# Edge lists by eighths, source gathers in two parts, longer expert jobs and late weights in a fused Mamba, attention and graph-routed expert kernel

## The chip, the cores and the metric

The kernel runs on one core of a Trainium2 chip. Its time is the device time of one execution in microseconds (us), the median of several runs. TensorE is called PE, VectorE DVE, ScalarE ACT, GpSimd POOL and SyncE SP, as in the profile; PEld is the weight load of PE.

## What is computed

The input x has 4 entries of 32 x 96 tokens (12288 tokens, 96 tiles of 128) with 256 features.

```python
# layer 0
x = x + mamba_d(mamba_t(group_norm(x)))          # selective scans along both axes
# layer 1
t = tokens(x)
t = t + attn(ln(t))      # additive attention inside each entry:
    h = tanh(q[:, :, None, :] + k[:, None, :, :] + bh); e = h @ Wa
    v = softmax(e) @ inputs
t = t + ffn(ln(t))       # a graph decides the experts of each token:
    h = (x @ W_gat).reshape(M, 4, 4); a_src, a_dst = (h*att_src).sum(-1), (h*att_dst).sum(-1)
    e = leaky_relu(a_src[src] + a_dst[dst])
    alpha = softmax of e over the edges of each dst
    agg = segment_sum(h[src] * alpha[:, :, None], dst) + b_gat
    scores = layernorm(agg).reshape(M, 4, 4).mean(1); top 2 of 4, softmax -> gates
    out = sum over experts of gate * (gelu(x @ W1 + b1) @ W2 + b2)
```

There are 1048576 edges with node numbers up to 65536, of which only 12288 are tokens. A source past the last token is read as the last token; edges to a destination past the last token do nothing. Each token also has an edge to itself.

## The kernel before

**Order of the work.** Layer 0 runs in blocks of 384 tokens, 48 slots to a block. When the first entry is through layer 0, the attention of entry 0 begins and is issued between the slots. `Attention.units` (line 866) goes over the tanh columns: 768 to an entry, 3072 in all, each one ACT instruction of 128x3072 (line 905) whose result PE reduces to scores (line 878). Three `th` buffers hold the results; the scores follow two columns behind. Twice per column the generator `steps` (line 2042) is advanced; it issues layer 0 first, and when that has ended, whatever else stands beside the last attention. `after` (line 1062) writes the normalised tokens, the table `tab_s` (20 numbers per token: 4 source scores, 16 features) and per entry `tab_a` (4 destination scores).

**Expert jobs beside layer 0.** `Beside` (line 1563) takes one job per block where `choose` (line 1591) permits: one expert on three half blocks of 256 tokens of an entry whose attention has ended. It uses the idle one of the two `krep` buffers for the weights and `qsel` for one half's input, which is loaded again by `fetch` for each half. The hidden products are issued at slots 0, 3, 5, 8, 10 and 12, the Gelu of all at slot 14 (line 1643), the outputs at slots 15 to 29. Results go to DRAM (`kept`). A unit is one block of 512 tokens by one of the 4 experts; there are 96.

**Edge lists.** `Edges.sort` (line 1192) runs on DVE beside the last attention, by a budget of 2.3 us of its own estimates per tanh column, none in one column of eight. It loads the edges in 32 pieces of 512 columns through two buffers (line 1226), keeps those with a token as destination, and compacts lists with `compact` (line 1138), some 50 short DVE instructions for a list of 384. The edges with both ends among the tokens end in one list of 384 per partition; it is split by four quarters of the destinations (an entry each) into lists of 108 columns. Edges from past the last token are counted by PE products (line 1322) instead. From then on one destination gather of 128 rows per column is issued on POOL (line 1127) for the first three quarters, after a copy that paces POOL (line 771). `Experts.early` (line 1735) does units of the first three entries on PE with a second budget per column, in pairs, by expert. The weights of all four experts, some 4.5 MB, are loaded when the lists are done (line 2069).

**The tail.** After the attention, `tail` (line 1821) issues a plan in half steps, six to an expert unit. For each group of 12 columns POOL gathers the sources (line 1425) and, for the last quarter, the destinations; a marker from DVE keeps POOL from running ahead of its half step (lines 1417 and 1418). `scores` and `values` make the weighted rows; `spread` makes one-hot matrices of the lane and of the quarter's 24 tiles and multiplies the latter by the rows (line 1469, 4 columns at a time); `place` adds them to a quarter's sums in PSUM, one PE product of 480 columns for each gathered column (line 1479). `finish` makes the gates of a quarter. Meanwhile the remaining units run (lines 1723 and 1731). A block whose expert outputs were stored is loaded again once its gates are there (2 MB, line 1881) with its tokens (line 1716), summed with the gates (line 1808) and written (line 1812).

Of the kernel before, what the change touches and what calls it, by code (L numbers as in the profile page):

```python
# [26 lines left out]
P = 128  # L27
# [4 lines left out]
KC = C // P  # L32
# [25 lines left out]
C2, CQ = 384, 108  # L58
# [3 lines left out]
HALVES = 3.0, 9.0  # L62
# [659 lines left out]
class Attention:  # L722
# [4 lines left out]
    def __init__(self, ctx, tc, ident, a, x1, x2, xn2T, tab_s, tab_a):  # L727
        self.nc = nc = tc.nc
        self.ident, self.x1, self.x2, self.xn2T = ident, x1, x2, xn2T
        self.tab_s, self.tab_a = tab_s, tab_a  # L730
# [331 lines left out]
    def after(self, b, t0=0, t1=NT):  # L1062
# [7 lines left out]
        for j in range(j0, N):  # L1070
# [26 lines left out]
            nc.sync.dma_start(self.tab_s[:, n0:n0 + CT, :], hb)  # L1097
            nc.sync.dma_start(self.tab_a[b][:, j * CT:(j + 1) * CT, :], db)
# [5 lines left out]
class Edges:  # L1104
# [6 lines left out]
    def __init__(self, ctx, tc, a, tab_a):  # L1111
        self.nc, self.tc, self.a, self.todo = tc.nc, tc, a, []
        self.tab_a, self.have, self.listed = tab_a, set(), False
        keep = ctx.enter_context(tc.tile_pool(name="el", bufs=1))
        new = lambda name, shape, dt=F32: keep.tile(shape, dt, tag=name, name=name)
        self.cnt = new("cnt", [P, NH])
        self.lost = new("lost", [P, 1])
        self.si, self.di = new("si", [P, 4, CQ], I32), new("di", [P, 4, CQ], I32)
        self.lane, self.tile = new("lane", [P, 4, CQ]), new("tile", [P, 4, CQ])
        self.lanes, self.tiles = new("lanes", [P, P]), new("tiles", [P, NH])  # L1120
        self.gd = new("gd", [P, 4, CQ, HEADS])
        self.nc.sync.dma_start(self.lanes, a["lanes"])

    def gather(self, q, c):
        if (q, c) not in self.have:
            self.have.add((q, c))
            self.nc.gpsimd.indirect_dma_start(  # L1127
                out=self.gd[:, q, c, :], out_offset=None,
                in_=self.tab_a[q].rearrange("p n f -> (p n) f"),
                in_offset=bass.IndirectOffsetOnAxis(ap=self.di[:, q, c:c + 1], axis=0))  # L1130
# [61 lines left out]
    def sort(self):  # L1192
# [4 lines left out]
        with ExitStack() as ctx:  # L1197
            kept = ctx.enter_context(tc.tile_pool(name="ek", bufs=1))
# [3 lines left out]
            with tc.tile_pool(name="es", bufs=1) as lists:  # L1202
# [4 lines left out]
                pair2, pairq, pair3 = new("pair2", C2, F32), new("pairq", C2, F32), new("pair3", 4 * CQ, F32)  # L1207
                over = new("over", 9, F32)
# [10 lines left out]
                with tc.tile_pool(name="ee", bufs=2) as pool:  # L1219
                    for q in range(4):  # L1220
                        for row, to, most in ((1, x, M), (0, s, M - 1)):
                            H = W1 // 4
                            for h in range(4):
# [21 lines left out]
                k1 = new("pair", 2 * W1)[:, :W1]  # L1245
# [3 lines left out]
                x2, _ = self.halves(pair2)  # L1249
                part, tl = w["keep"][:, :C2], w["keep"][:, C2:2 * C2]  # L1250
                for q in range(4):
                    v.tensor_scalar(tl, x2, 7, None, ALU.logical_shift_right)
                    v.tensor_scalar(part, tl, float(P + q * NT), None, ALU.is_ge)
                    v.scalar_tensor_tensor(part, tl, float(P + (q + 1) * NT), part, ALU.is_lt, ALU.mult)
                    v.tensor_copy(pairq, pair2)
                    yield 1.5
                    yield from self.compact(w, part, pairq, CQ, pair3[:, q * CQ:(q + 1) * CQ],
                                            over[:, 5 + q:6 + q])
                v.tensor_reduce(self.lost, over, AX.X, ALU.max)


                n = 4 * CQ
                flat = lambda t: t.rearrange("p q c -> p (q c)")
                x3, s3 = self.halves(pair3)
                lo, hi, d = w["go"][:, :n], w["move"][:, :n], w["bit"][:, :n]
                for of, rows in ((s3, self.si), (x3, self.di)):
                    v.tensor_scalar(d, of, VALID - 1, None, ALU.bitwise_and)
                    v.tensor_scalar(lo, d, P - 1, None, ALU.bitwise_and)
                    v.tensor_scalar(lo, lo, float(NH), None, ALU.mult)
                    v.tensor_scalar(hi, d, 7, None, ALU.logical_shift_right)  # L1270
                    if rows is self.di:
                        v.tensor_scalar(lo, lo, float(NT) / NH, None, ALU.mult)
                        for q in range(1, 4):
                            part = hi[:, q * CQ:(q + 1) * CQ]
                            v.tensor_scalar(part, part, float(-q * NT), 0.0, ALU.add, ALU.max)
                    v.tensor_tensor(flat(rows), lo, hi, ALU.add)
                    yield 1.5
# [4 lines left out]
                self.listed = True  # L1282
# [14 lines left out]
            yield 1.0  # L1297
            p = ctx.enter_context(tc.tile_pool(name="eo", bufs=3))
            ps = ctx.enter_context(tc.tile_pool(name="ep", bufs=1, space=PSUM))
            pc = ps.tile([P, NH], F32, tag="pc", name="pc")  # L1300
            starts = [q * W2 + g for q in range(4) for g in range(0, C1, G1)]
# [32 lines left out]
class Graph:  # L1334
# [85 lines left out]
    def gather(self, j, u):  # L1420
        nc, ed = self.nc, self.ed
        if j not in self.got:
            self.got[j] = self.wk.tile([P, GP, ROW], F32, tag="gs", name="gs", bufs=6)
        q, c0 = divmod(j * GP, CQ)
        nc.gpsimd.indirect_dma_start(  # L1425
            out=self.got[j][:, u, :], out_offset=None, in_=self.tab_s.rearrange("p n f -> (p n) f"),
            in_offset=bass.IndirectOffsetOnAxis(ap=ed.si[:, q, c0 + u:c0 + u + 1], axis=0))
        ed.gather(q, c0 + u)

    def scores(self, j):  # L1430
        nc = self.nc
        gs = self.got.pop(j)
        q, c0 = divmod(j * GP, CQ)
        gd = self.ed.gd[:, q, c0:c0 + GP, :]
        e = self.wk.tile([P, GP, HEADS], F32, tag="e", name="e")
        sh = self.wk.tile([P, GP, HEADS], F32, tag="sh", name="sh")
        v = self.wk.tile([P, GP, ROW], F32, tag="v", name="v", bufs=4)
# [6 lines left out]
        self.got[j], self.v[j] = gs, v  # L1444

    def values(self, j):

        v = self.v[j]
        self.nc.vector.tensor_tensor(
            v[:, :, :HF].rearrange("p n (h x) -> p n h x", x=NEXP),  # L1450
            self.got.pop(j)[:, :, HEADS:].rearrange("p n (h x) -> p n h x", x=NEXP),
            v[:, :, HF:].unsqueeze(3).to_broadcast([P, GP, HEADS, NEXP]), ALU.mult)

    def spread(self, j, g):

        nc, ed = self.nc, self.ed
        q, c0 = divmod(j * GP + g * GG, CQ)
        cols = slice(c0, c0 + GG)
        ol = self.wk.tile([P, GG, P], F32, tag="ol", name="ol")
        oh = self.wk.tile([P, GG, NT], F32, tag="oh", name="oh")  # L1460
        rh = self.wk.tile([P, GG, NT, ROW], F32, tag="rh", name="rh")
        for to, among, which in ((ol, ed.lanes, ed.lane),
                                 (oh, ed.tiles[:, q * NT:(q + 1) * NT], ed.tile)):
            n = to.shape[2]
            nc.vector.tensor_tensor(to, among.unsqueeze(1).to_broadcast([P, GG, n]),
                                    which[:, q, cols].unsqueeze(2).to_broadcast([P, GG, n]),
                                    ALU.is_equal)
        v = self.v[j][:, g * GG:(g + 1) * GG, :]
        nc.vector.tensor_tensor(rh, oh.unsqueeze(3).to_broadcast([P, GG, NT, ROW]),
                                v.unsqueeze(2).to_broadcast([P, GG, NT, ROW]), ALU.mult)  # L1470
        return ol, rh

    def place(self, j, g, ol, rh):
        nc = self.nc
        q, c0 = divmod(j * GP + g * GG, CQ)
        if c0 == 0:
            self.pa[q] = self.ps.tile([P, JB], F32, tag="pa", name="pa")
        for u in range(GG):
            nc.tensor.matmul(self.pa[q][:, :NT * ROW], ol[:, u, :],
                             rh[:, u].rearrange("p n f -> p (n f)"),  # L1480
                             start=(c0 + u == 0), stop=(c0 + u == CQ - 1))
# [81 lines left out]
class Beside:  # L1563
# [5 lines left out]
    PRODUCTS = {0: (0, 0), 3: (0, 1), 5: (1, 0), 8: (1, 1), 10: (2, 0), 12: (2, 1)}  # L1569
    GELU = 14  # L1570
    OUTPUTS = {15: (0, 0), 17: (0, 1), 20: (1, 0), 23: (1, 1), 26: (2, 0), 29: (2, 1)}

    def __init__(self, ctx, tc, a, l0, att, xn2T, dram):
# [7 lines left out]
        n = TOK // self.half // 3  # L1581
# [3 lines left out]
    def units(self):  # L1585

        halves = {(2 * (b * TOK // TB) + 3 * j + k, e) for b, e, j in self.done for k in range(3)}
# [3 lines left out]
    def choose(self, last):  # L1591
# [9 lines left out]
        self.w1, self.w2 = expert_places(place)  # L1601
        rest = att.qsel[(att.entry + 1) % 2]
# [5 lines left out]
        self.first = 2 * (b * TOK // TB) + 3 * j  # L1608
        self.fetch(0)

    def fetch(self, k):
        m = (self.first + k) * self.half
        self.nc.sync.dma_start(self.xt, self.xn2T[:, :, m:m + self.half].rearrange("k p m -> p k m"))

    def __call__(self, slot, last):
        nc = self.nc
        if self.job:
# [3 lines left out]
            if slot - 1 in self.PRODUCTS:  # L1621
                k, f2 = self.PRODUCTS[slot - 1]
                for f in (2 * f2, 2 * f2 + 1):
                    nc.vector.tensor_scalar(self.h[:, k, f, :], self.ps[:, f % 2, :],
# [7 lines left out]
            if slot in self.PRODUCTS:  # L1632
# [6 lines left out]
                if f2 and k < 2:  # L1639
                    self.fetch(k + 1)  # L1640
            if slot == self.GELU:
                h = self.h.rearrange("p k f m -> p (k f m)")
                nc.scalar.activation(h, h, AF.Gelu)
            if slot in self.OUTPUTS:
                k, q = self.OUTPUTS[slot]
                self.ps = self.bank()
                for f in range(FC):
                    nc.tensor.matmul(self.ps[:, 0, :], self.h[:, k, f, q * P:(q + 1) * P],  # L1648
# [15 lines left out]
class Experts:  # L1664
# [25 lines left out]
    def weights(pool, nc, a):  # L1690
        w1 = pool.tile([P, NEXP, KC, FF], F32, tag="w1", name="w1")
        w2 = pool.tile([P, NEXP, FC, C], F32, tag="w2", name="w2")
        for e in range(NEXP):
            nc.sync.dma_start(w1[:, e], a["W1"][e].rearrange("(k p) f -> p k f", p=P))
            nc.sync.dma_start(w2[:, e], a["W2"][e].rearrange("(k p) f -> p k f", p=P))
        b1 = pool.tile([P, NEXP, FC], F32, tag="b1", name="b1")
        nc.sync.dma_start(b1, a["b1"])
# [119 lines left out]
    def outputs_tile(self):  # L1817
        return self.io.tile([P, NQ, NEXP, C], F32, tag="all", name="all")


def tail(tc, a, ed, ex, w, tab_s, tab_a, gates):


    with ExitStack() as ctx:
        gr = Graph(ctx, tc, a, ed, tab_s, tab_a, gates)
# [12 lines left out]
        PQ, PG = CQ // GP, GP // GG  # L1838

        h = free = 0.0  # L1840
        for m in range(4 * PQ):
            q = QUARTERS[m // PQ]
            j = q * PQ + m % PQ
            wide = HALVES[q == B - 1]
            for u in range(GP):
# [344 lines left out]
```

## Time and profile before

| | |
|---|---|
| time, median of 3 runs (lowest, highest) | 15007.42 us (15002.35, 15027.46) |
| the profiled execution, its span | 15006.76 us, 15004.8 us |
| busy: PE, DVE, ACT, POOL | 11632.7, 10437.2, 12227.7, 9042.6 us |
| last tanh of the attention starts | 13868.1 us |
| jobs beside layer 0 (Gelu of line 1643) | 25 of three halves, 5620.8 to 10987.8 us |
| first destination gather | 11883.4 us |
| gathers before and after 13940 us | 324, 540 |
| last gather | 14789.7 us |
| early units, units of the tail | 22, 37 |
| stored blocks loaded in the tail | 19 of 2 MB |

The strips of the page divide the span into 40 slices; a digit is the busy share in tenths. A window answer gives for a stretch its length and the busy time and number of instructions of PE, PEld, DVE, ACT and POOL, then the clock that PE was granted, the share of DMA time and GB/s. A row of a group has the line, the engine, what is written from what, the count, the busy time with the mean in ns, and behind the second bar the idle time of that engine just before these instructions, with what ended it. PE's 4-byte products have two records for each product.

### The profile page before, as it was taken

The page shows a single profiled execution, that of the slowest core. Times are in us where ns is not written, and L with a number is a line of the kernel's source. Part 1 is how long each engine was busy: PE and PEld are TensorE (multiplying, and loading weights), DVE is VectorE, ACT ScalarE, POOL GpSimd, SP SyncE. Part 2 cuts the span into 40 slices and gives each one's busy share as a digit, 9 for nine tenths or more (in the row PEclk, how much of TensorE's full clock was granted, in tenths as well). Part 3 has the DMA queues.
Part 4 walks back from the last instruction along what each step waited for, and adds up shares of the span by engine and source line. Part 5 has one row for each costly group of instructions (what it writes and reads, how often), then busy time and mean ns, then how long its engine had stood idle before and what let it go on. Part 6 is the DMA issues. An engine that isn't in the chain of part 4 may idle for free.

```text
span 15004.8 us, 223310 instructions
## 1 busy us (share of the span) xinstructions
PE 11632.7 (78%) x86496; PEld 5146.9 (34%) x86496; DVE 10437.2 (70%) x14862; ACT 12227.7 (81%) x9485; POOL 9042.6 (60%) x6971
## 2 busy tenths in 40 slices
PE   5676656777777778888887787888877888888888
PEld 2333322222222323333333333333333344433544
DVE  7888887777777877777777877577767633311367
ACT  3454538999999889999999899999988899999121
POOL 5777777777777777767676677477640144100683
PEclk8988978888888888899999889899988999999999
DMA  6777764445454544555454444355531000000224
GB/s 207 227 230 233 239 203 142 150 151 153 150 152 153 161 152 147 152 149 153 150 154 156 149 150 152 105 153 151 152 115 44 15 16 10 24 23 23 59 54 136
DMA packets 1197826, 1986.83 MB, mean 132 GB/s; under 512 B 411984, under 2 KB 645072, under 8 KB 1194320
## 3 DMA queue, kind: packets, MB, share of 16 engines
q1 hardware_dynamic: 1169104, 1967.10, 42.8%
q0 software_dynamic: 27648, 5.36, 0.7%
q8 instruction: 680, 11.14, 0.3%
q14 instruction: 394, 3.23, 0.1%
HBM read 1864.71 MB, written 107.35 MB: 131 GB/s over the span
## 4 chain that ended last, share of the span: by engine, by line
ACT 17%; PE 16%; DVE 7%; POOL 5%; issue 4%; DMA 1%; SPq 0%; DVEq 0%; ACTq 0%; POOLq 0%
ACT th L905 12%; PE pe L878 8%; POOL gs L1425 3%; PE pv L984 3%; ACT dA L410 2%; DVE h L448 1%; ACT pr L968 1%; POOL gd L1127 1%; PE ptw L975 1%; PE po L1731 1%; PE pz L517 1%; PE pc L1322 1%; DVE y L1808 0%; PE ex L1648 0%; DVE dB L423 0%
## 5 line engine op out<-in xcount | busy, mean ns | idle before, releaser
L905 ACT ACTIVATE th<-krep,qsel 128x3072 f32<-128x3072 f32 x3072 | 8667.0, 2847 | 377.0 <-PE pe L878 359.0
L878 PE MATMUL pe<-th,wa_blk 128*32 128x384 f32 x49152 | 5050.1, 539 | 1587.7 <-ACT pr L968 1361.7
L455 POOL TENSOR_TENSOR h<-h,bC 128x768 f32<-128x768 f32 x2048 | 3759.8, 1837 | 2586.0 <-DVE h L448 2187.4
L448 DVE TENSOR_TENSOR_SCAN h<-dA,dB 128x384 f32<-128x384 f32 x3008 | 2707.8, 942 | 988.7 <-ACT dA L410 717.2
L878 PEld LDWEIGHTS pe<-th,wa_blk 128*32 128x32 f32 x49152 | 1459.3, 116 | 4154.1 <-issue 1974.4
L423 DVE TENSOR_TENSOR dB<-bB,dtu 128x768 f32<-128x768 f32 x1912 | 1811.9, 948 | 172.0 <-ACT dtu L498 137.2
L462 POOL TENSOR_TENSOR h<-h 128x768 f32<-128x768 f32 x752 | 1419.6, 1888 | 53.6
L410 ACT ACTIVATE dA<-dt,t_A 128x380 f32<-128x380 f32 x2048 | 1124.7, 570 | 386.2 <-DVE h L448 296.5
L474 PE MATMUL py<-h,ident 128*128 128x384 f32 x2176 | 944.7, 567 | 490.8 <-POOL h L455 490.7
L410 ACT ACTIVATE dA<-dt,d_A 128x372 f32<-128x372 f32 x2048 | 1102.3, 562 | 146.4 <-DVE h L443 107.9
L984 PE MATMUL pv<-xn,pT 128*32 128x257 f32 x18432 | 1101.0, 387 | 129.5 <-DVE pT L977 128.7
L1043 POOL TENSOR_SCALAR sf<-sel,f 128x32 f32<-128x32 f32 x384 | 144.7, 398 | 1583.9 <-ACT f L1039 1481.5
L443 DVE TENSOR_TENSOR_SCAN h<-dA,dB 128x768 f32<-128x768 f32 x544 | 948.3, 1751 | 153.2 <-ACT dA L410 87.7
L977 DVE COPY pT<-ptw 128x512 f32<-128x512 f32 (+1 forms) x768 | 419.3, 546 | 738.3 <-PE ptw L975 737.8
L984 PEld LDWEIGHTS pv<-xn,pT 128*32 128x32 f32 x18432 | 580.2, 111 | 704.9 <-DVE pT L977 256.1
L464 POOL TENSOR_TENSOR y<-y,h 128x384 f32<-128x384 f32 x752 | 783.2, 1042 | 59.0
L463 POOL TENSOR_TENSOR h<-h 128x384 f32<-128x384 f32 x752 | 780.7, 1038 | 58.9
L474 PEld LDWEIGHTS py<-h,ident 128*128 128x128 f32 x2176 | 427.1, 212 | 970.1 <-POOL h L455 740.3
L961 DVE TENSOR_REDUCE nb<-pe 128x1 f32<-128x768 f32 x384 | 362.4, 944 | 405.7 <-PE pe L878 405.6
L1425 POOL DMA_INDIRECT gs<-tab_s,si x432 | 517.5, 1198 | 108.4 <-issue 108.4
L986 DVE COPY pvs<-pv 128x257 f32<-128x257 f32 x384 | 160.7, 419 | 603.4 <-PE pv L984 601.9
L1127 POOL DMA_INDIRECT gd<-tab_a,di x432 | 448.8, 1039 | 185.1 <-issue 182.0
(291 smaller groups left out, 15267.6 us busy)
## 6 DMA issues: line engine op xcount, KB each, us to landing
bB<-bc SPq DMA_DIRECT2D x2048, 384.0 KB
bC<-bc SPq DMA_DIRECT2D x2048, 384.0 KB
all<-kept SPq DMA_DIRECT2D x19, 2048.0 KB
x<-x SPq DMA_DIRECT2D x144, 256.0 KB
x<-x SPq DMA_DIRECT2D x192, 128.0 KB
xt<-xn2T SPq DMA_DIRECT2D x41, 512.0 KB
kept<-ko SPq DMA_DIRECT2D x39, 512.0 KB
qsel<-xn2T SPq DMA_DIRECT2D x75, 256.0 KB
```

The lines of the kernel that those rows point to most:

```text
L410: nc.scalar.activation(inner(dA[:, s * T:(s + 1) * T] if alone else self.dA[s][:, :T]), inner(blk["dt"][:, e, :]), AF.Exp, scale=blk["w"][ ...
L423: nc.vector.tensor_tensor(dB, blk["bB"].pop(j), z["dtu"].unsqueeze(1).to_broadcast([P, SB, T]), ALU.mult)
L443: nc.vector.tensor_tensor_scan(flat(h), dA[:, :SB * T], flat(dB), 0.0, ALU.mult, ALU.add)
L448: nc.vector.tensor_tensor_scan(h[:, s, :], self.dA[s][:, :T], dB[:, s, :], 0.0, ALU.mult, ALU.add)
L455: nc.gpsimd.tensor_tensor(h, h, blk["bC"].pop(j), ALU.mult)
L462: nc.gpsimd.tensor_tensor(h0, h0, h1, ALU.add)
L464: nc.gpsimd.tensor_tensor(y[e], y[e], h0[:, 0, :], ALU.add)
L474: nc.tensor.matmul(z["py"], self.ident, h[:, s, :], start=(i == 0), stop=(i == DS - 1))
L878: nc.tensor.matmul(pe[q * QU:(q + 1) * QU, j, :KQ // 2], self.wa[:, k, :], th[:, c0:c0 + KQ // 2], start=(k == 0), stop=(k == NK - 1))
L905: nc.scalar.activation(th, s["krep"], AF.Tanh, bias=s["qsel"][:, col:col + 1])
L984: nc.tensor.matmul(pv[q * QU:(q + 1) * QU, :C + 1], pT[:, i, q * QU:(q + 1) * QU], s["xn"][:, q * NK + i, :], start=(i == 0), stop=(i == N ...
L1425: nc.gpsimd.indirect_dma_start(out=self.got[j][:, u, :], out_offset=None, in_=self.tab_s.rearrange("p n f -> (p n) f"), in_offset=bass.Ind ...
```

## The change

Five things are changed together.

- The expert jobs beside layer 0 take four halves instead of three: 12 jobs to an entry, 24 in all. The fourth half's hidden values lie in the unused part of `krep`. The products are at slots 0, 2, 4, 6, 8, 10, 11, 13, the Gelu at 15 in two instructions, the outputs at each even slot from 16 to 30.
- The edges come in 64 pieces. The list of 384 is first split by the source: one list of 112 with sources in the last entry, one of 280 with the others; both, in this order, are then split by eighths of the destinations (12 tiles each) into lists of 60 columns. Sources of the last entry may stand only in the first 24 columns; otherwise the edges count as lost.
- A second table `tab_e` holds the rows of the first three entries. Beside the last attention, the destination gathers of six eighths and then the source gathers of columns 24 to 59 of the eighths 6, 7, 4, 5, 0 and 1 are issued, one and two at a time in turn.
- In the tail the product into the sums has 240 columns; the groups of 12 take 0.3 half steps for each gather that is still wanted, at least 1.5; the stored blocks are loaded in two halves of 1 MB, 4 half steps and 1 half step ahead, where it was all of it 8 ahead.
- The weights of all experts are loaded at the start of the tail.

```diff
-C2, CQ = 384, 108
+C2, CL, CY = 384, 112, 280
+N8, T8, CE, LATE = 8, 12, 60, 24
+EARLY = 6, 7, 4, 5, 0, 1
-HALVES = 3.0, 9.0
+HALVES = 1.5, 0.3
 ...
+            if b < B - 1:
+                nc.sync.dma_start(self.tab_e[:, n0:n0 + CT, :], hb)
 ...
+    def early(self, k, c):
+        self.have.add((k, c, "s"))
+        self.indirect(self.eg[:, EARLY.index(k), c - LATE, :], self.tab_e, self.si[:, k, c:c + 1])
+    def columns(self):
+        first = [(self.gather, k, c) for k in range(N8 - 2) for c in range(CE)]
+        return first + [(self.early, k, c) for k in EARLY for c in range(LATE, CE)]
 ...
-                            H = W1 // 4
-                            for h in range(4):
+                            H = W1 // 8
+                            for h in range(8):
 ...
-                for q in range(4):
-                    v.tensor_scalar(tl, x2, 7, None, ALU.logical_shift_right)
-                    ...
-                    yield from self.compact(w, part, pairq, CQ, pair3[:, q * CQ:(q + 1) * CQ],
-                                            over[:, 5 + q:6 + q])
+                for some, cap, to, n in ((last, CL, pairs[:, :CL], 5), (rest, CY, pairs[:, CL:], 6)):
+                    v.tensor_copy(pairq[:, :C2], pair2)
+                    yield 0.5
+                    yield from self.compact(w, some, pairq[:, :C2], cap, to, over[:, n:n + 1])
+                for k in range(N8):
+                    ...
+                    yield from self.compact(w, part, pairq, CE, pair3[:, k * CE:(k + 1) * CE],
+                                            over[:, 8 + k:9 + k])
 ...
-    PRODUCTS = {0: (0, 0), 3: (0, 1), 5: (1, 0), 8: (1, 1), 10: (2, 0), 12: (2, 1)}
-    GELU = 14
-    OUTPUTS = {15: (0, 0), 17: (0, 1), 20: (1, 0), 23: (1, 1), 26: (2, 0), 29: (2, 1)}
+    HALVES = 4
+    PRODUCTS = dict(zip((0, 2, 4, 6, 8, 10, 11, 13), ((k, f) for k in range(4) for f in range(2))))
+    GELU = 15
+    OUTPUTS = dict(zip(range(16, 32, 2), ((k, q) for k in range(4) for q in range(2))))
 ...
     def outputs_tile(self):
-        return self.io.tile([P, NQ, NEXP, C], F32, tag="all", name="all")
+        return self.io.tile([P, 2, NEXP, C], F32, tag="all", name="all")
 ...
+        w = Experts.weights(ctx.enter_context(tc.tile_pool(name="late2", bufs=1)), tc.nc, a)
 ...
-            at(2 * t - 8, fetch)
+            at(2 * t - 4, lambda fetch=fetch: fetch(0))
+            at(2 * t - 1, lambda fetch=fetch: fetch(2))
 ...
-                    if columns is None and ed.listed:
-                        columns = [(q, c) for q in range(B - 1) for c in range(CQ)]
+                    if columns is None and ed.listed and att.normed >= B - 1:
+                        columns, turn = ed.columns(), 1
                     if columns:
                         att.pace()
-                        ed.gather(*columns.pop(0))
+                        turn = 3 - turn
+                        for f, k, c in columns[:turn]:
+                            f(k, c)
```

## The prediction

> **What bounds the kernel now.** I read the utilisation strips first, for the stages.
>
> ```profile
> PE   5676656777777778888887787888877888888888
> DVE  7888887777777877777777877577767633311367
> ACT  3454538999999889999999899999988899999121
> POOL 5777777777777777767676677477640144100683
> ```
>
> One slice is 375 us. From slice 7 to 36 ScalarE (ACT) stands at 8 or 9: the tanh of line 905, 3072 times 2.85 us, is the pace of layer 0 with attention beside it and of the last attention entry. In the last three slices it falls to 1 or 2, and PE, POOL and DVE are high instead: the tail. So there are two accounts: what the attention stages lose, and what the tail wins. For the tail I asked for busy times by window, cut where the destination gathers end (14257) and where all gathers end (14790), and then for POOL's groups:
>
> ```profile
> 13942.00:14257.00 315.00, 278.00 (x824) 161.57 (x823) 108.39 (x231) 62.68 (x84) 260.77 (x295) 0.94 0.23 50
> 14257.00:14790.00 533.00, 465.87 (x1269) 248.27 (x1268) 393.46 (x791) 121.20 (x146) 445.16 (x407) 0.94 0.25 67
> 14790.00:15005.00 215.00, 172.03 (x534) 109.96 (x532) 152.82 (x327) 32.57 (x45) 1.13 (x2) 0.90 0.49 164
> ```
>
> ```profile
> L1425 POOL DMA_INDIRECT gs<-tab_s,si x432 | 517.5, 1198 | 108.4 <-issue 108.4
> L1127 POOL DMA_INDIRECT gd<-tab_a,di x108 | 121.1, 1121 | 32.9 <-issue 32.9
> L1418 POOL COPY seen<-mark 1x1 f32<-1x1 f32 x162 | 68.4, 422 | 5.4 <-DVE mark L1417 4.6
> ```
>
> Columns after the length: PE, weight load, DVE, ACT, POOL, clock, DMA share, GB/s. Busy plus idle of POOL's three rows is 854 us, all of 13942 to 14790: the indirect gathers run back to back, and 37.6% of the chain of waits from 13800 on is line 1425. The tail's first 848 us are POOL's, with PE close behind; the last 215 us are 10 expert units and the gated sums of stored outputs, where the DMA runs at 164 GB/s. The tail's other prices:
>
> ```profile
> L1479 PE MATMUL pa<-rh,ol 128*128 128x480 f32 x864 | 403.3, 617 | 100.0 <-DVE rh L1469 57.0 <-DVE mark L1417 43.0
> L1731 PE MATMUL po<-w,h 128*128 128x256 f32 x1184 | 284.8, 397 | 39.9 <-DVE o L1798 34.9 <-DVE ko L1795 5.0
> L1723 PE MATMUL ph<-xt,w 128*128 128x512 f32 x580 | 264.9, 592 | 0.0
> L1469 DVE TENSOR_TENSOR rh<-oh,v 128x1920 f32<-128x1920 f32 x108 | 233.5, 2162 | 3.7
> L1808 DVE SCALAR_TENSOR_TENSOR y<-all,gates,y 128x256 f32<-128x256 f32 x304 | 143.7, 484 | 34.8 <-DMA y<-x 23.0 <-issue 3.7
> ```
>
> One gathered column costs PE 403.3/432 = 0.93 us; one unit (a block by an expert, 37 of them) (284.8+264.9)/37 = 14.9 us.
>
> **The tail, term by term.** *Gathers.* Before, 540. After, 480 columns need 480 source and 480 destination gathers; beside the last attention go 6x60 = 360 destination and 6x36 = 216 source gathers, so 384 stay: 168 for quarter 3, 48 each for quarters 2 and 0, 120 for quarter 1. A mark costs (68.4+5.4)/162 = 0.455 us. Taking 81 marks from each of the first two windows, a gather costs (315-37)/216 = 1.29 us, then (533-37)/324 = 1.53 us while DVE is busier. *Units.* The list-expert jobs now take four halves. The Gelu of line 1643 shows when jobs ran: 13 in entry 1, 12 in entry 2. The new list has 12 of entry 0 and 12 of entry 1, so all 24 fit: 48 units instead of 37. The early units have a budget per tanh column that does not change; I take 22 again. The tail keeps 96-48-22 = 26 units instead of 37.
>
> The planned half steps (six to a unit) become 50 for quarter 3, 47 for quarters 2 and 0, 36 for quarter 1, then 58 to the last stored block.
> - Quarter 3, POOL: 168x1.29 + 51x0.455 = 240 us (PE only some 180).
> - Quarters 2 and 0: POOL needs 96x1.53 + 30x0.455 = 161. PE needs 47/6 units x 14.9 = 117 and 240 columns at half the width, so 0.46 us (a 256-wide product of line 1731 takes 284.8/592 = 0.48): 110; together 227. DVE comes to some 220: 60 spreads of half of 2.16 plus 0.9, and scores, gates and sums. Two engines near full in program order: 250.
> - Quarter 1, POOL: 120x1.53 + 36x0.455 = 200.
> - The rest: 12 stored blocks of 3 MB and 5 units. 36 MB at the 200 to 250 GB/s of the busiest stretches is 150 to 190; the prefetch is now half a block, so I take 175; between 130 and 235, the old 215 with two exposed loads.
> - Weights (4.5 MB) behind the last attention store at 13909.5; the early units hold PE until 13934.5, which covers some 20 us of loading. They were loaded when the lists were done; now their ten SP issues (0.5 us each by the issues of that queue there) and 4.5 MB stand ahead of the source table `hall`, which the first reduction, and through it POOL's first instruction of the tail, waits for. What stays of that is +8. With the cover gone, +25; at best 0.
>
> Sum 240+250+200+175+8 = 873 against 1063: **-190** (bounds -110 and -270).
>
> A row behind the gather price: its median is 0.97 us, its mean 1.20. The Trainium skill, SBUF — State Buffer, SBUF: two separate sides, says that VectorE operations that take the shared port keep GpSimd from writing descriptors. The trace agrees in direction (1.29 at 34% DVE, 1.53 at 74%); by the rule the shorter spreads would give part of that back. If every gather took its median and the 0.26 us between gathers (141.3/540), quarters 3 and 1 would lose 168x0.06 + 120x0.30 = 46 us. The sum does not use it.
>
> **Layer 0 with attention.** The Ln of line 354 comes once a block: six blocks from 2780.8 without a job take 181 us each, six from 5739.6 with one 193.6; in entry 2 it is 186.4 without and 191.4 with. So a job costs 5 to 12.5, say 9 us; 2.6 of it are two table loads, so a half costs 2.1. After: 24x(9+2.1) - 25x9 = +41. The fourth half's input is fetched one slot (4 us) ahead, not two: it lands in about 4 us, and PE already waited 26.6 us for 50 such fetches. I add 1 us a job: **+65**. Low end, the Gelu alone (2.76/3 x 21 halves): +19. High end, 12.5 us a job and a whole 4 us wait on PE: +165.
>
> **The lists.** DVE is full while they are made, and a tanh column then takes 3.8 us, against 3.0 after:
>
> ```profile
> 11800.00:11900.00 100.00, 76.95 (x705) 32.16 (x704) 85.63 (x247) 76.74 (x32) 9.50 (x16) 0.88 0.07 20
> 11900.00:12000.00 100.00, 90.20 (x962) 42.19 (x961) 39.09 (x73) 96.11 (x39) 42.80 (x71) 0.95 0.05 7
> ```
>
> The second row is after the lists: ACT rises from 77 to 96 of 100 us. The waits for edge pieces in that stage:
>
> ```profile
> DVE pair L1229 <- DMA e<-in_edges: 28.7, 18, 2.6
> ```
>
> Four compactions of 384 become two of 384 and eight of 392. The code's own budget grows from 411 to 476; at 2.3 a column, seven columns in eight, that is 35 more slow columns: 35x0.8 = +28. The edges come in 64 pieces instead of 32, two in flight, so a burst drains faster than it fills: the 28.7 us of waits grow by as much, of which I put 22 on the path. **+50**; 0 if ACT hides all, +130 if the 102 us of new DVE work (six compactions of 17) and the waits all show.
>
> The Trainium skill, DMA: Bandwidth & Descriptors, Anatomy of one DMA — SWDGE (gpsimd) path, speaks against small pieces: each transfer pays about 2.0 us whatever its size. These pieces are issued by SP; by that figure 32 more, two in flight, would be an estimated 32 us.
>
> The 576 early gathers go at 1.5 a column: 384 columns of the 560 left, and 1.5x0.97+0.18 = 1.6 us of POOL's 3.0; POOL stands at 0 to 4 tenths there, so nothing waits. If they did, each would be back in the tail at 1.3. The second table store is 36 issues of 0.33 us on SP: hidden.
>
> **Sum.** The profiled execution took 15006.8 (span 15004.8); the median of the three runs is 0.7 above, no difference here. 15006.8 - 190 + 65 + 50 = 14932, say **14935**.
>
> **Rivals.** *The attention stages hide what is added* (20%): ACT pays its Gelus (+19), the lists +15, the stored blocks run at the DMA's 150: 15007-215+34 = 14826. For it: ACT idles only 5% beside layer 0. Against: blocks with jobs are 5 to 12 us longer where the Gelu explains 5. *Slower: the one-slot fetch* (22%). SP issues in order, and its waits hold:
>
> ```profile
> SPq L373 <- POOL h L455: 1312.4, 375, 10.7
> ```
>
> A broadcast waiting for POOL, up to 10.7 us, stands ahead of the fetch of slot 10; PE, in order, then holds the tanh scores of slot 11. From 3.1 us of further loss a job (75/24) the gain is gone; at 6.5 us it is 15090. Against: three th buffers cover one column. *It does nothing measurable* (16%): the attention stages give back 160 to 220 of the 190: 15007. That the change misses its own aim, early gathers not done or jobs not fitting, the counts above exclude.
>
> **Chances.** Forecast 42%, 14880 to 14976. Faster by over 0.2% (30 us, about what a measurement can tell here): 42+20 = 62%; within 16%; slower 22%. Range 14790 to 15090: from the lower rival, less 36 us more of the tail's bound (-250), to the slower one at its price.
>
> **What would show it.** POOL: 384 gathers after the attention, last one some 690 us after the tail's start (848 now). Line 1643: 24 jobs, blocks with a job at 193 to 196 us. Last tanh at 13868+115. The rows of pa halve in width. Wrong if a wait for qsel tops PE's list beside layer 0, if DVE stands on edge pieces by more than 80 us, or if the tail's first product waits for weights.

## The result and the profile after

The changed kernel takes 15103.75 us (median of 4 runs, 15083.18 to 15115.51); the kernel before, beside it, 15004.89 (14998.33 to 15027.46). The ratio is 1.0062 [1.0044, 1.0079]: 0.62% slower. The forecast was 14935, and the time lies above the range's 15090. The profiled execution took 15102.04 us, span 15099.2. (All experiments below give their ratio against the kernel before, run on the same chip; it took 15008 to 15011 us beside the first eight.)

Three instants of the trace cut the difference into the prediction's own terms. The first block of layer 0 with an expert job starts (its Ln, line 356 now). The first edge piece is asked for (line 1226 before), which in both kernels comes while tanh column 2216 is the last to have started: layer 0 has ended, and the lists begin. The last tanh of the attention starts (line 907 now). The stretch between the first two is called the stretch of the jobs below.

| | before | after | difference | predicted |
|---|---|---|---|---|
| first block with a job starts | 5547.5 | 5562.6 | +15 | 0 |
| from there to the first edge piece | 5567.2 | 5797.4 | +230 | +65 |
| from there to the last tanh | 2753.4 | 2825.7 | +72 | +50 |
| from the last tanh to the end of the span | 1136.7 | 913.5 | -223 | -190 |
| span | 15004.8 | 15099.2 | +94.4 | -75 |

The 15 us ahead of the first job are the spread of single executions: e3 below, which is the same kernel up to there, reaches that block at 5549.6, and all runs lie between 5547.5 and 5565.5.

So the tail gave more than forecast, the lists cost some 20 us more than forecast, and the miss is in layer 0 with attention: 230 us, above even the high bound of 165. The strips of the changed kernel (tenths of busy time in slices of 377 us):

```profile
PE   5666756777777778788887777888886778888886
DVE  7888887777777877777777877577766763331257
ACT  3454539999999889988989899999897889999621
POOL 5777777777777666666667676466660025540164
```

In the last two slices, which hold most of the tail, POOL stands at 6 and 4, and in the last DVE is highest. Beside layer 0 ACT has an 8 in several slices where it had a 9. The tail by windows from 14320 on, cut where the last destination gather ends (14506), where the last gather ends (14921) and where PE ends (15000); columns as before (length; PE, weight load, DVE, ACT, POOL; clock, DMA share, GB/s):

```profile
14320.00:14506.00 186.00, 143.19 (x510) 101.99 (x508) 60.21 (x159) 36.98 (x47) 150.88 (x175) 0.90 0.19 38
14506.00:14740.00 234.00, 201.24 (x784) 154.99 (x785) 189.85 (x478) 67.87 (x87) 131.87 (x131) 0.93 0.21 54
14740.00:14921.00 181.00, 151.90 (x564) 112.19 (x563) 153.70 (x380) 50.93 (x62) 145.99 (x155) 0.94 0.43 125
14921.00:15000.00 79.00, 65.42 (x234) 46.41 (x232) 62.37 (x148) 17.25 (x22) 0.37 (x1) 0.91 0.44 144
15000.00:15100.00 100.00, 0.00 (x0) 0.00 (x0) 65.46 (x139) 0.00 (x0) 0.00 (x0) 0.52 0.74 256
```

In the first row POOL is the fullest (151 of 186 us), from 14506 to 14740 PE is (201 of 234), then PE and DVE are level (152 and 154 of 181), and in the last 100 us only DVE and the loads of stored blocks are left, at 256 GB/s. POOL's groups in the tail, count and mean in ns behind the name, and idle time behind the second bar:

```profile
L1129 POOL DMA_INDIRECT gs<-tab_s,si x192 | 220.4, 1148 | 49.5 <-issue 49.5
L1129 POOL DMA_INDIRECT gd<-tab_a,di x120 | 131.9, 1099 | 31.7 <-issue 31.7
L1129 POOL DMA_INDIRECT gs<-tab_e,si x72 | 81.8, 1136 | 18.8 <-issue 18.8
L1459 POOL COPY seen<-mark 1x1 f32<-1x1 f32 x119 | 38.6, 325 | 89.0 <-DVE mark L1458 88.5
```

192+120+72 = 384 gathers, as forecast, and POOL, which had waited 5 us for marks, now waits 89: behind quarter 3 it is no longer what holds the tail.

Beside layer 0 I asked for the waits in one stretch of entry 1 with jobs, 5770 to 7850 us. Each row: who waited for whom, us in total, times, longest. First before, then after:

```profile
ACT th L905 <- PE pe L878: 56.9, 58, 3.8
...
PE ex L1637 <- DMA qsel<-xn2T: 10.1, 10, 1.8
```

```profile
ACT th L907 <- PE pe L880: 151.7, 66, 8.8
...
PE ex L1688 <- DMA qsel<-xn2T: 49.7, 11, 6.2
```

ACT, which sets the pace there, waits 95 us more for PE's tanh scores within 2080 us, and PE 40 us more for an expert half's input. One of these waits in the timeline of the changed kernel (start, length, engine, instruction, idle time before it):

```profile
5818.74 1.99 PE L1688 MATMUL ex<-qsel,krep 128*128 128x256 f32 x8
...
5822.33 0.32 SPq L375 DMA_DIRECT2D bC<-bc  x1
5822.60 5.59 ACT L907 ACTIVATE th<-krep,qsel 128x3072 f32<-128x3072 f32 x2
5822.74 0.38 SPq L375 DMA_DIRECT2D bB<-bc  x1
5823.22 0.38 SPq L1661 DMA_DIRECT2D qsel<-xn2T  x1
...
5828.11 3.75 PE L1688 MATMUL ex<-qsel,krep 128*128 128x256 f32 x8 [5.21 <-DMA qsel<-xn2T]
...
5836.10 2.86 ACT L907 ACTIVATE th<-krep,qsel 128x3072 f32<-128x3072 f32 x1 [6.95 <-PE pe L880]
```

The third half's products (slot 10) free the input's place at 5820.73. The fetch of the fourth half is issued 2.5 us later, behind two broadcasts on SP, and lands 4.9 us after its issue (taken from PE's start; over the 22 such waits of the trace it is 4.1 to 5.9 us, median 5.0). PE stands 5.21 us, then runs 3.75 us of products, and only then the tanh scores; ACT, two columns further on in the meantime, idles 6.95 us. The Trainium skill (SBUF — State Buffer, The DMA setup-cost knee) gives a transfer about 2 us and its bytes at 436 GB/s; for the 256 KB of a fetch that is an estimated 2.6 us, and the trace shows 4.9 here.

### The profile page after: what moved, and what is told of

Same layout as the page of the kernel before. It is cut to its first block, busy times and chain, and to the rows that moved or that the text cites. A ratio compares the mean times of both kernels' runs of the same rounds, so it can differ in the third digit from the quotient of the medians.

```text
span 15099.2 us, 224705 instructions
## 1 busy us (share of the span) xinstructions
PE 11476.5 (76%) x86736; PEld 5210.4 (35%) x86736; DVE 10510.5 (70%) x15387; ACT 12221.9 (81%) x9466; POOL 9070.8 (60%) x7084
## 4 chain that ended last, share of the span: by engine, by line
ACT 36%; PE 28%; DVE 18%; issue 8%; POOL 6%; DMA 2%; SPq 0%; DVEq 0%; POOLq 0%; ACTq 0%
ACT th L907 25%; PE pe L880 12%; ACT dA L412 6%; PE pv L986 4%; DVE h L445 3%; DVE h L450 3%; DVE dB L425 2%; POOL h L457 2%; ACT pr L970 2%; PE pz L519 2%; PE ex L1688 1%; PE ptw L977 1%; PE px L238 1%; PE po L1783 1%; PE py L476 1%
## 5 line engine op out<-in xcount | busy, mean ns | idle before, releaser
L1129 POOL DMA_INDIRECT gd<-tab_a,di x480 | 500.1, 1042 | 162.7 <-issue 159.4
L977 PE MATMUL ptw<-ident,pr 128*128 128x128 f32 x2304 | 476.6, 324 | 126.0 <-DVE pT L979 59.2
```

## The experiments

My theory after the result: each job's fourth half costs layer 0 far more than 2.1 us, by three things, the fetch (the slower rival of the prediction), PE's products before the tanh scores, and ACT's second Gelu; the lists and the tail do what was forecast. The rival theory: the loss is the fetch's alone.

Stage times are those of one profiled execution of each kernel. Most lie within 6 us of the kernel's median, but those of e2, e5, e9 and e10 lie 20, 15, 11 and 16 us above it and that of e3 18 us below, so differences of times are given beside them. The seven kernels with three halves that add nothing that delays a job (before, e3, e6, e7, e8, e10, e11) take 5557 to 5575 us for the stretch of the jobs; that is the spread against which the others are read. A table of all runs stands at the end of this section.

**e1_slot9.** One product of the third half goes a slot earlier, so that the fetch has two slots again, as before.

```diff
-    PRODUCTS = dict(zip((0, 2, 4, 6, 8, 10, 11, 13), ...
+    PRODUCTS = dict(zip((0, 2, 4, 6, 8, 9, 11, 13), ...
```

> The changed kernel with the sixth product of a job at slot 9 instead of 10, so that the fourth half's input is asked for two slots ahead of its product at slot 11, not one. Same work, same number of slots. Theory A (the wait of PE for that input, 4.6 us a job, and what stands behind PE, is most of the 10 us that a block with a job became longer): blocks with a job fall from 202 to 195 or 196 us, the wait of PE for qsel falls to the 1 us a job of before, the time falls by 120 to 170 us to 14935 to 14985. Theory B (the work of the fourth half itself, 7.6 us of PE and 2.8 us of DVE in slots that were already nearly full): the wait goes, but other waits take its place; blocks stay at 199 us or more, the time falls by less than 70 us.

15018.0 us, 1.0007 [0.9997, 1.0017]; last tanh 14107.4, 78 earlier than in the changed kernel. The same stretch of waits:

```profile
ACT th L907 <- PE pe L880: 104.2, 67, 3.9
...
PE ex L1688 <- DMA qsel<-xn2T: 5.5, 3, 3.0
```

The wait for qsel is nearly gone (49.7 to 5.5 us), and ACT's wait has fallen back by half of its increase. The stretch of the jobs is 75 us shorter than in the changed kernel, the time 86. This lies between the theories: the fetch is real, but blocks with a job still take 200.3 us (median), where theory A had 195 or 196.

**e2_two_inputs.** The input gets a second place in the unused part of `krep`, and the fetches run two halves ahead.

```diff
+        self.xts = [t.rearrange(...) for t in (rest[:, :n], place[:, KC * FF + FC * C + n:])]
         self.fetch(0)
+        self.fetch(1)
 ...
-                if f2 and k + 1 < self.HALVES:
-                    self.fetch(k + 1)
+                if f2 and k + 2 < self.HALVES:
+                    self.fetch(k + 2)
```

> The changed kernel with two places for a job's input (the second half of the unused part of krep is the second), so that every half's input but the first two is asked for one half's products ahead; slots as in the changed kernel. Theory A: PE waits for qsel almost nowhere, blocks with a job at 194 to 196 us, the time at 14920 to 14985. Theory B: blocks at 199 us or more, the time above 15035.

15012.9 us, 1.0001 [0.9992, 1.0011]; last tanh 14121.0, 65 earlier. No wait for qsel is left in the stretch, and ACT still waits 112.2 us for PE. The stretch of the jobs is 78 us shorter than in the changed kernel, the time 91. Two ways of taking the fetch's wait away agree; with it gone the change is worth nothing.

**e3_three_halves.** The changed kernel with the class `Beside` of the kernel before: lists, early gathers and tail stay, the jobs have three halves.

```diff
-    HALVES = 4
-    PRODUCTS = dict(zip((0, 2, 4, 6, 8, 10, 11, 13), ...
+    PRODUCTS = {0: (0, 0), 3: (0, 1), 5: (1, 0), 8: (1, 1), 10: (2, 0), 12: (2, 1)}
-    GELU = 15
+    GELU = 14
```

> The changed kernel with the expert jobs of before (three halves, slots of before); lists, gathers, late weights and tail as changed. Both theories: blocks with a job as before (192 us), last tanh near 14186-254 = 13932; the tail has up to 11 units more, which cost 100 to 165 us there. Time 14945 to 15010. If the attention stage does not come back, the loss was not the jobs'.

14935.6 us, 0.9951 [0.9935, 0.9968]. Blocks with a job take 192.1 us again (192.1 before, 202.3 in the changed kernel; medians), and the stretch of the jobs 5562.5, as before. The last tanh is at 13938.8, 71 later than before, the tail takes 976.5, 160 less than before. The rest of the change without the fourth half (lists, early gathers, late weights) is faster; the fourth half alone makes the change a loss. It takes 11 units off the tail (913.5 against 976.5: -63, where 100 to 165 were expected) and puts 247 us ahead of it, 235 of them in the stretch of the jobs (by the two times, 168 us apart, it is 231 ahead of the tail).

**e4_before_four.** The counterpart: the kernel before with four halves (the reverse of e3's diff on `Beside`).

> The kernel before with the four-half jobs alone. Both theories: last tanh 240 to 260 us later than before (near 14120); POOL still gathers 540 times in the tail, so that the units saved shorten only the stretch after the last gather, by 50 to 110 us. Time 15150 to 15210. If it is below 15100, the jobs' price was not what the changed kernel lost, or the gathers were not the tail's bound.

15204.7 us, 1.0132 [1.0115, 1.0149]; last tanh 14089.5, +221. The stretch of the jobs grows by 214. Here the tail shrinks by only 27, from 1137 to 1110, less than the 50 to 110 expected: its 540 gathers hold it until 15013, and in the 187 us behind them PE is busy 22.7. Where POOL sets the tail, units taken off PE bring little.

**e5_pe_twice.** On e3, PE issues the products and outputs of the third half twice: PE's part of a fourth half with no fetch, Gelu or VectorE work.

```diff
-                for f in (2 * f2, 2 * f2 + 1):
+                for f in (2 * f2, 2 * f2 + 1) * (1 + (k == 2)):
 ...
-                for f in range(FC):
+                for f in (*range(FC),) * (1 + (k == 2)):
```

> The three-half jobs on the changed kernel (e3_three_halves), with the products and outputs of the third half issued twice on PE, into the same places: PE's work of a fourth half (7.6 us a job) and nothing else of it; no second input, no more DVE, ACT or DMA work. Without the wait for the input, a fourth half still cost some 7 us a block (199 against 192). Theory P (PE is near full in the slots of the job, and what is added there is added to the block): blocks with a job near 198 us, last tanh 110 to 170 us after that of e3_three_halves (13939), time 15040 to 15110. Theory D (it is the DVE's six short evictions and sums, in order with the scans, or ACT's second Gelu): blocks stay within 2 us of 192, time below 14985.

15021.0 us, 1.0011 [1.0001, 1.0021]. The stretch of the jobs takes 5659.4 us, 97 more than in e3, over 25 jobs 3.9 us each (84 to 102 against the whole spread of kernels with three halves); the two times are 85 us apart. (The last tanh, at 14059.2, is 120 us after e3's, but the two profiled executions lie 15 above and 18 below their medians.) The time is between the theories' figures and nearer to P's. The waits of ACT in the same stretch, e3 and then e5:

```profile
ACT th L907 <- PE pe L880: 55.3, 54, 3.8
```

```profile
ACT th L907 <- PE pe L880: 103.3, 96, 3.8
```

The 48 us come in 42 more waits, none longer than before: so the added products delay the scores behind them a little at many places.

**e6_dve_twice.** On e3, VectorE's evictions and sums of the third half are issued twice.

```diff
+                for _ in range(1 + (k == 2)):
+                    nc.vector.tensor_tensor(o, self.ps[:, 0, :], self.b2, ALU.add)
```

> The three-half jobs on the changed kernel, with DVE's evictions and bias sums of the third half issued twice: the 2.8 us of DVE a job that a fourth half adds, and no PE, ACT or DMA work. Theory P: blocks within 2 us of 192, time 14925 to 14975. Theory D: blocks at 196 us or more, time above 15010.

14928.9 us, 0.9945 [0.9929, 0.9962]: no cost in the time, and blocks with a job at 191.8 us (median). VectorE has room for this work beside layer 0.

**e9_gelu_more.** On e3, a further Gelu of one half (128x1024) in each job, into a part that nothing reads.

```diff
+                nc.scalar.activation(self.spare, self.h[:, 0].rearrange("p f m -> p (f m)"), AF.Gelu)
```

> This is the kernel of e3_three_halves with one more Gelu of a half (128x1024, about 1 us of ScalarE) in each of its 25 jobs, written into the part of krep that the job does not use. Theory A (ScalarE's row paces these blocks, as the chain of waits through tanh and exp says, so what is left of the loss after the fetch and TensorE's fourth half is ScalarE's): the last tanh moves from 13939 by 20 to 35 us, the time from 14936 to 14955 to 14975. Theory B (ScalarE's Gelu lies in gaps in which it waits for TensorE): both stay within 8 us, and the rest of the loss is denser products in the attention's slots.

15068.4 us, 1.0021 [1.0011, 1.0031]. Neither this time nor the last tanh can be set beside e3's: with this kernel and the next two the kernel before itself took 15039.37 us, and e10 and e11, which up to the tail are instruction for instruction e8, take 2881 and 2879 us from the first edge piece to the last tanh where e8 took 2806. Most of that lies where the early gathers run: in 500 us there (12614 to 13114 in e8, 12717 to 13217 in e10) the granted clock is 0.94 and 0.91, ACT is busy 481 and 448 us and waits 18.9 and 42.7 us for PE's scores. Why the clock was lower is not known. The stretch of the jobs does not show it: 5575.1 and 5557.4 us in e10 and e11, 5559 to 5574 in e3, e6, e7 and e8. There e9 takes 5609.9, so 35 to 53 us more, which is 1.4 to 2.1 us a job; the Gelu itself takes 1.06 in the trace. That fits the first theory: what is added to ACT there is added in full to the path, if not more.

**e7_no_early_sources.** On e3, no source gathers beside the last attention.

```diff
-        return first + [(self.early, k, c) for k in EARLY for c in range(LATE, CE)]
+        return first
```

> The three-half jobs on the changed kernel, without the source gathers beside the last attention: 600 gathers in the tail instead of 384. If POOL's gathers are the tail's bound, each costs 1.3 to 1.5 us: last gather 280 to 320 us later; the expert units then lie beside them, so that the stretch after the last gather (243 us in e3_three_halves) shrinks to some 100; time 15070 to 15150. The rival, that the shorter products and not the moved gathers made the tail shorter: less than 60 us above e3_three_halves.

15024.9 us, 1.0013 [1.0003, 1.0023], so the 216 early source gathers are worth 89 us, less than I had expected. The last gather starts at 14885.5 instead of 14659.8, 226 us later, but the stretch behind it shrinks from 256 to 144: units that had waited there lie beside the gathers.

**e8_three_pieces.** On e3, three buffers for the edge pieces instead of two.

```diff
-                with tc.tile_pool(name="ee", bufs=2) as pool:
+                with tc.tile_pool(name="ee", bufs=3) as pool:
```

> The three-half jobs on the changed kernel, with three places for edge pieces in flight instead of two. DVE waited 53 us for 64 pieces (28.7 us for 32 before). If these waits are on the path of the attention, as the prediction took it, they fall by a half and the time falls by 15 to 30 us to 14905 to 14920; if ACT hides them, the time stays within 8 us of e3_three_halves.

14889.7 us, 0.9923 [0.9906, 0.9939], the best of all kernels here. VectorE's wait for pieces over the whole span falls from 52.6 to 28.8 us, and from the first edge piece to the last tanh it takes 2806 us instead of 2827, so these waits were on the path; the last tanh comes 25 us earlier (13914.2). The times differ by 46 us, more than the 15 to 30 expected; of that, 18 come from e3's profiled execution being so far below its median, and nothing here explains them. Changed kernel, VectorE's waits from 11350 to 12330:

```profile
DVE pair L1244 <- DMA e<-in_edges: 53.1, 37, 2.7
```

That is 37 waits of up to 2.7 us for pieces of 128 KB, where there were 18 for pieces twice as large.

**e10_wide and e11_wide_late.** On e8, more half steps beside each gather of the tail; e11 also issues scores, values and spreads three half steps later.

```diff
-HALVES = 1.5, 0.3
+HALVES = 1.5, 0.4
```

> This is the kernel of e8_three_pieces with more half steps of the experts laid beside each gather of the tail (HALVES from the plan's value to 1.5 and 0.4), so that units move from the stretch behind the last gather, where TensorE alone sets the end, to the stretch in which GpSimd's gathers do. Theory A (TensorE has room beside the gathers, since it waits there for rh and for mark): 20 to 50 us less than 14890, thus 14840 to 14870. Theory B (the gathers' own chain is lengthened by what is put beside it, or TensorE is already full there): within 10 us of 14890.

> This is e10_wide with the scores, values and spreads of a tail unit issued three half steps later than now (h+7, h+8, h+9), so that TensorE does not stand in order before an rh that VectorE has not made yet. Theory A (TensorE's waits for rh cost the tail its time): a further 10 to 30 us below e10_wide. Theory B (the gathers set that stretch): the same as e10_wide within 8 us.

14983.6 us, 0.9963 [0.9950, 0.9975], and 14996.6 us, 0.9975 [0.9965, 0.9984], above e8. Since the stage ahead of the tail differs as said under e9, only the tails can be compared: behind the last tanh they take 980.6 and 994.4 us, in e8 975.4. But e9, run beside them, has the plan of e3 and e8 in its tail and takes 1004.4 us for it, where e3 takes 976.5. So against e8 there is no gain, against e9 there is one of 24 and 10 us, and whether the wider plan helps stays open. The tail's windows in e8, cut at the last gather, and then in e10:

```profile
13914.00:14635.00 721.00, 588.78 (x2233) 425.52 (x2234) 433.76 (x1077) 189.81 (x229) 468.42 (x508) 0.92 0.29 76
14635.00:14890.00 255.00, 223.21 (x774) 149.93 (x772) 156.71 (x341) 47.48 (x66) 0.42 (x2) 0.96 0.44 149
```

```profile
14017.00:14838.00 821.00, 686.91 (x2551) 490.84 (x2550) 466.49 (x1180) 210.66 (x256) 483.04 (x547) 0.92 0.30 81
14838.00:14998.00 160.00, 134.16 (x456) 90.67 (x454) 124.45 (x278) 30.41 (x41) 0.38 (x1) 0.94 0.55 190
```

98 us of PE's work moved ahead of the last gather, that stretch grew by 100 us, and the one behind it shrank by 95. PE is busy 812 us of 976 in e8's tail, POOL 469. That PE and not POOL sets the tail with three halves fits this; it was not tried by itself.

All runs, in us; the last three columns are of the profiled execution:

| run | time | profiled | stretch of the jobs | first edge piece to last tanh | tail |
|---|---|---|---|---|---|
| before | 15007.4 | 15006.8 | 5567 | 2753 | 1137 |
| changed | 15103.8 | 15102.0 | 5797 | 2826 | 914 |
| e1_slot9 | 15018.0 | 15021.3 | 5722 | 2829 | 911 |
| e2_two_inputs | 15012.9 | 15032.4 | 5719 | 2843 | 910 |
| e3_three_halves | 14935.6 | 14917.1 | 5562 | 2827 | 976 |
| e4_before_four | 15204.7 | 15200.8 | 5781 | 2760 | 1110 |
| e5_pe_twice | 15021.0 | 15035.8 | 5659 | 2838 | 975 |
| e6_dve_twice | 14928.9 | 14930.3 | 5574 | 2829 | 971 |
| e9_gelu_more | 15068.4 | 15079.2 | 5610 | 2898 | 1004 |
| e7_no_early_sources | 15024.9 | 15030.9 | 5569 | 2826 | 1075 |
| e8_three_pieces | 14889.7 | 14891.8 | 5559 | 2806 | 975 |
| e10_wide | 14983.6 | 14999.3 | 5575 | 2881 | 981 |
| e11_wide_late | 14996.6 | 14992.5 | 5557 | 2879 | 994 |

## Why the prediction was wrong

**The step that failed** is the one in "Layer 0 with attention" that says "so a half costs 2.1". It took a job's whole price, 9 us less 2.6 for table loads, and divided it by three halves: a mean price for what is a further piece of work. With "I add 1 us a job" for the fetch, a block with a job was to become 3.1 us longer; it became 10 us longer (192.1 to 202.3). Three halves and their Gelu together had cost 9 us; that they lie in gaps of PE and the fourth does not is the reading that fits, but no run takes one of the three away. The runs give the fourth half's parts as follows, of some 244 us: the 235 between the changed kernel's stretch of the jobs and e3's, and some 9 that one job fewer saves.

| part of the fourth half | run | us |
|---|---|---|
| PE's products and outputs, 3.9 us x 24 jobs | e5 | 93 |
| the input fetched one slot ahead | e1, e2 | 75 to 78 |
| ACT's second Gelu, 1.4 to 2.1 us x 24 | e9 | 34 to 50 |
| VectorE's evictions and sums | e6 | 0 |
| not separated | | 23 to 42 |

Each figure is uncertain by some 10 us, by the spread of the kernels with three halves. In the last row lie the other slots of the products and outputs, which were not tried by themselves (e5 issues its added products in the slots of the third half); that the parts simply add up is assumed. The fetch's 75 to 78 us over 24 jobs are 3.1 to 3.3 each for the 1 us of the step: "it lands in about 4 us" was short too, as it took 4.1 to 5.9 after its issue and was issued late. And the high bound of +165 let only one of the two be large: it paired 12.5 us a job with a whole 4 us wait, and did not ask what PE's own 8.4 us of a half do to the scores queued behind them (in the stretch of waits above its product rows are busy 179.6 us for 41 halves and its output rows 162.6 us for 40).

**The slower rival** had its mechanism right and its time nearly (15090 against 15104), but not its share: the fetch is about a third of the loss, 3.1 to 3.3 us a job where its price took 6.5 beyond the 1 us of the sum, so that its time came near is luck. Without it the change is even (e1, e2), not faster. Its place was as described: PE, in order, holds the tanh scores of slot 11, and the fetch stands behind broadcasts on SP. What I held against it, "three th buffers cover one column", does not hold: in the timeline above ACT runs 5.59 us of tanh while PE is away, and PE's wait and products together are 9 us.

**The rival "the attention stages hide what is added"** is out: ACT idles only 4.5% of the stretch before the change, and what is added to it there shows in full (e9).

**The tail** was right, term by term. From the first gather (14269) to the last destination gather of quarter 3 (14506) it took 237 us where 240 were forecast; quarters 2 and 0 took 232 where 250 were, quarter 1 183 where 200 were, the rest 178 where 175 were. It ran 26 units, as counted beforehand. The whole tail gave -223 for -190, inside the bounds; the largest misses are the two engines "near full in program order" and POOL's price in quarter 1. PE needed 0.50 us for a half-wide column where 0.46 was taken. The first product waits 5.3 us, by the trace for its input behind the late weights, within the +8. What the sum did not see is how its two gains depend on each other. In the tail the lists and early gathers alone bring 160 us (e3), the 11 units alone 27 (e4), and together 223: only after POOL's gathers are out of the way do fewer units count for more, and then at 63/11 = 5.7 us each, not at the 14.9 us that one costs PE.

**The lists** cost +72 for +50, inside the range of 0 to 130. The doubled waits for edge pieces that the term spoke of are there (28.7 to 53.1 us), below the 80 named as a sign of error; 20 to 25 us of the term are theirs (e8). The rest was not taken apart. (By the term's own figures the longer budget is 65/2.3 x 8/7 = 32 slow columns, not 35, which is 2 us.)

**Of the signs named beforehand**, 384 gathers, 24 jobs and half-wide pa rows came as said, the last gather some 650 us after the first instead of some 690. The blocks with a job at 202.3 us instead of 193 to 196, and the last tanh at +318 instead of +115, show the failed step directly. The wait for qsel is not at the top of PE's list in the stretch (49.7 us; the waits for ACT are larger), and still it counted, since what it delays is the pacing engine.

## What to carry to other kernels

Price a further piece of work on a nearly full in-order engine at what it pushes back on the pacing engine, not at the mean price of the pieces that already lie there, which may have taken the gaps. Before work is moved out of a stage, ask what sets that stage once the other part of the change has acted, and what the work is worth there: here 11 units were worth 63 us in the tail and cost some 235 beside the attention. A shortened prefetch is counted from the moment its place comes free, with what stands ahead of it on its queue, to its landing.

## What was not expected of the hardware

- A fetch of 256 KB landed 4.9 us after its issue on SP (4.1 to 5.9 over 22 waits), while all transfers together ran at 242 GB/s in those 6 us and at 146 GB/s in the stretch around it; with the 2.5 us that it stood behind broadcasts, the place was empty for 7.4 us.
- Added PE work of a half (16 products of 128x256) made a job 3.9 us longer in many waits none longer than 3.8 us, though PE had been busy for only 1720 of the stretch's 2080 us (e3).
- The same instructions took 75 and 73 us longer from the first edge piece to the last tanh in e10 and e11 than in e8, at a granted clock of 0.91 and 0.90 instead of 0.94 in the 500 us compared, while the stretch of the jobs agreed within 18 us. So times of kernels that were not run together can differ by 0.5% for the same work.
